# Three middle taps of R from two shared products: their sum and difference added at eviction, the sums of S on GpSimd, T3 as a scalar_tensor_tensor

## The chip, the core and the metric

The kernel runs on one core of a Trainium2 chip, in one launch, everything in float32. The metric is the device time of a run in microseconds; the kernel before took 473.57 us (median of three runs, 473.06 to 473.9). TensorE (PE) multiplies, VectorE (DVE), ScalarE (ACT) and GpSimd (POOL) do the elementwise work, SyncE (SP) issues most DMAs. SBUF holds the tiles, PSUM the results of matmuls.

## The reference, cut to what matters

Four one-dimensional convolutions without a nonlinearity between them, their weights modulated by a style vector per sample, then the residual. 128 samples, 64 channels, 1024 columns.

```python
def _layer(x, style, w, b, mw, mb, typ):
    s = style @ mw.T + mb
    weight = SCALE * w * s[:, None, :, None]
    demod = lax.rsqrt(jnp.sum(weight * weight, axis=(2, 3)) + EPS)
    weight = weight * demod[:, :, None, None]
    if typ == 'same':
        out = jax.vmap(_conv_same)(x, weight) + b[None, :, None]
    elif typ == 'upsample':
        out = jax.vmap(_conv_up)(x, weight.transpose(0, 2, 1, 3)) + b[None, :, None]
        out = _blur(out, 2.0 * blur_k, (1, 1))
    elif typ == 'downsample':
        xb = _blur(x, blur_k, (2, 2))
        out = jax.vmap(_conv_down)(xb, weight) + b[None, :, None]
    return out
...
out = x
for i, typ in enumerate(('same', 'upsample', 'same', 'downsample')):
    out = _layer(out, style, weights[i], biases[i], mod_w[i], mod_b[i], typ)
x = x + out
```

## The kernel before, in words

The four layers are linear, so the kernel first multiplies their weights into one convolution of nine taps per sample (`Wf`, three planes of three taps) and then applies it to x, which is read in three interleaved planes of 342 columns. Four samples are a quad; 32 quads, q = 0 to 31. On the 128 partitions two samples lie one above the other, and a group of four matmuls of 64 rows by 64 columns (two row halves, two column halves) does one tap for all four samples.

**Composing the weights of a quad** has three stages, each a matmul chain into PSUM, then a copy with the sample's scale:

- stage 1 (`stage1_a`, `stage1_b`, L429): the last layer's weights times the third's, in PSUM `psS`. The tile S gets slots 0 to 3 by ScalarE (L400), slots 4 and 5 by VectorE (L482), and GpSimd finishes slot 2 (L485).
- stage 2 (`share`, `stage2_rest`, L507): S times E, the blurred second layer's nine taps, into `psR`: seven blocks of 64 columns. ScalarE evicts them with the scale tC into the tile R (L400, 128x448, one for each row half), and `r_sums` (GpSimd, L639) adds two pairs of R's blocks into R's slots 7 and 8.
- stage 3 (`stage3_b`, `stage3_a`, L622): R times the first layer's weights, in `psA` and `psW`, evicted by ScalarE into `Wf`. VectorE then forms H, the combinations of taps that a fast convolution needs: `combine_a` (H1, L713; the residual's identity in the middle tap, L710, twice; h3, L713) and `combine_b` (three L713).

**The inputs of a quad** (T04, T12, T3) are combinations of x's planes: G by VectorE (`in_g01`, `in_g2`, L713), T3 by VectorE (`in3`, L762), T04 by VectorE (`in04`, L793), the two halves of T12 by GpSimd (`in1` L779, `in2` L784). **The five products** conv0 to conv4 (L814) are twelve matmuls of 342 columns each into `psA` or Y; VectorE's `sum1` (L713) and `sum2` (L713 into Y, L873 into y) combine them, ScalarE writes the outputs (L893).

**Shared products.** Two products of S's sums occur in several blocks of R. `share_sums` (VectorE, L502) adds two pairs of S's slots; `share` multiplies them by E in three groups into a free part of `psA`; `share_copy` (ScalarE, L530) copies the two results, each into two blocks of `psR`, and `stage2_rest` adds the rest of R, 14 groups, on top.

**The order.** Each engine executes its own instructions in the order in which the program writes them; semaphores connect the engines. The prologue has four turns (`early_turn`), then `turn_of(q)` runs for q = 4 to 28, then an epilogue. A turn works on several quads at once, n = q + 1, c = q + 2, s = q + 4: R of quad c, conv2 of q, `r_sums(c)`, `sum2(q)`, `in2(n)`, stage 3 of c, `combine_a(n)`, conv4(q), `combine_b(n)`, conv3(n), stage 1 of s, `in04(n)`, conv0(q), `in_g01(c)`, `share(c + 1)`, conv1(n), `sum1(n)`, `in3(c)`, `in1(c)`. `sharing(q)` holds for q = 5 to 27, 23 turns; only these have the shared products. The tile R has two buffers, S four; `psR`, `psS` and `psW` share one pair of PSUM banks.

Of the kernel before, what the change touches and what calls it, by code (L numbers as in the profile page):

```python
# [48 lines left out]
F32 = mybir.dt.float32  # L49
# [5 lines left out]
C = 64  # L55
# [8 lines left out]
def kernel(  # L64
# [424 lines left out]
    whole, shared_ps = {}, {}  # L489
    later = wsq.rearrange("c l k o -> c (l k) o")  # L490
    Ed, Wd = later[:, :6], later[:, 6:8]

    def tap_differences():

        d = Ed[:, :4].rearrange("c (a b) o -> c a b o", a=2)
        for b in range(2):
            nc_g.tensor_sub(d[:, :, b], E[:, 4 * b : 4 * b + 5 : 4], E[:, 2:7:4])
        nc_g.tensor_sub(Ed[:, 4:], E[:, 3:8:4], E[:, 5:6].to_broadcast([P, 2, C]))

    def share_sums(q):  # L500
        t = whole[q]
        nc_v.tensor_add(t[:, :, 6:8], t[:, :, 1:5:3], t[:, :, 2:6:3])  # L502

    def chain_matmul(dst, weight, st, slots, last=False):
        for r, rows in enumerate(HALF):
            for c, cols in enumerate(HALF):
# [4 lines left out]
                    start=False,  # L511
# [4 lines left out]
    def share(q, ps):  # L516

        at = [NB + 4 + i * C for i in range(3)]
        p12, p34 = ([b[:, i:j] for b in ps] for i, j in zip(at, at[1:]))
        chain_matmul(p12, E[:, 2], chain[q], slice(6, 7))  # L520
        chain_matmul(p34, E[:, 6], chain[q], slice(6, 7))
        chain_matmul(p34, E[:, 5], chain[q], slice(7, 8), True)
        shared_ps[q] = [b[:, at[0] : at[2]] for b in ps]

    def share_copy(q):

        ps = unit(ps_w, f"psR{q}")
        for r in range(2):
            src = shared_ps[q][r].rearrange("c (a o) -> c a o", a=2)
            nc_a.copy(  # L530
                ps[r][:, C : 5 * C].rearrange("c (a b o) -> c a b o", a=2, b=2),
                src[:, :, None, :].to_broadcast([P, 2, 2, C]),
            )
        shared_ps[q] = ps

    def stage2_rest(q):

        ps = shared_ps.pop(q)
        block = lambda i, n=1: [b[:, i * C : (i + n) * C] for b in ps]
        apart = [b[:, : 4 * C].rearrange("c (a b o) -> c a b o", a=2, b=2)[:, :, 0] for b in ps]  # L540
        plan = (
            (apart, E[:, 0], slice(1, 4, 2)),
            (block(1), Ed[:, 0], slice(2, 3)),
            (block(2), Ed[:, 1], slice(1, 2)),
            (block(3), E[:, 2], slice(3, 4)),
            (block(3), Ed[:, 2], slice(2, 3)),
            (block(4), Ed[:, 3], slice(1, 2)),
            (block(4), E[:, 4], slice(3, 4)),
            (block(5, 2), E[:, 8], slice(2, 4)),
            (block(5), E[:, 6], slice(3, 4)),  # L550
            (block(1, 2), E[:, 1], slice(4, 6)),
            (block(2), E[:, 3], slice(4, 5)),
            (block(3), Ed[:, 4], slice(5, 6)),
            (block(4), Ed[:, 5], slice(4, 5)),
            (block(5), E[:, 7], slice(5, 6)),
        )
        for n, (dst, weight, slots) in enumerate(plan):
            chain_matmul(dst, weight, chain[q], slots, n == len(plan) - 1)
        return ps

    def stage2(q, pool=None, engs=(nc_a, nc_a), between=None):
        if q in shared_ps:
# [8 lines left out]
        for r in range(2):  # L571
            scaled_copy(engs[r], flat(t[:, r, :7]), ps[r][:, : 7 * C], tC[:, q, r : r + 1])
# [186 lines left out]
    def in3(q, pairs=BOTH_PAIRS):  # L759
        if q < NQ:  # L760
            X, t = Xs[q % NX], t_tile(q, "T3")
            nc_v.tensor_sub(t[:, pairs, 0, :NJ], plane(X, 3, pairs), plane(X, 1, pairs))  # L762
# [32 lines left out]
    def columns(groups, n):  # L795

        for g in groups:
            for i in range(2) if g < n else (None,):
                yield g, slice(0, NB) if i is None else slice(NB // 2 * i, NB // 2 * (i + 1))

    PIECES = {(0, 3): 3, (0, 1): 3, (0, 2): 3, (1, 3): 2}

    def product(q, m, ps, groups=range(K), alone=False):
# [3 lines left out]
        for g, at in columns(groups, PIECES.get((q, m), 0)):  # L807
            for s, rows in enumerate(HALF):
                for c, cols in enumerate(HALF):
# [4 lines left out]
                    nc.tensor.matmul(  # L814
# [931 lines left out]
```

## Time and profile before

| | before |
|---|---|
| median of 3 runs | 473.57 us (473.06 to 473.9) |
| the profiled execution | 472.43 us |
| its span | 470.6 us |
| instructions | 26974 |
| DMA | 70.79 MB, mean 150 GB/s |
| granted clock of TensorE | 1.00 |

The span is the time from the first to the last instruction that the profiler recorded; the profiled execution's own time is 1.83 us longer. A row of the timeline reads: start in us, duration in us, engine, line of the kernel, operation, output <- input, shape; in square brackets the idle time of the engine before it and what ended it. A row of a line's summary reads: count, then the shortest, median and longest duration in ns. PEld is the load of weights into TensorE, which runs beside its matmuls. In the chain of waits, each piece is a start, a duration and what ran.

### The profile page before, as it was taken

To read this page: it belongs to the slowest core of one execution; us is meant where nothing else is said; L and a number is where in the kernel's file an instruction comes from. 1 tells how busy PE (TensorE), PEld (TensorE's weight loads), DVE (VectorE), ACT (ScalarE), POOL (GpSimd) and SP (SyncE) were. 2 spreads that over 40 slices of the span, in tenths; PEclk is the share of its full clock that TensorE was granted. 3 is DMA by queue.
4 is the path that set the end of the run, shared out by engine and by line. 5 is a ranking of instruction groups with operands and counts; after the bars stand their busy time and mean duration, and the time that the engine had idled before them with its cause. 6 is when DMAs were issued, how large, how long until landed. Compare 5 with 4: busy or idle time off the path is not lost.

```text
span 470.6 us, 26974 instructions
## 1 busy us (share of the span) xinstructions
PE 465.3 (99%) x12036; PEld 339.3 (72%) x12036; DVE 413.4 (88%) x677; ACT 317.9 (68%) x759; POOL 178.4 (38%) x219
## 2 busy tenths in 40 slices
PE   9999999999999999999999999999999999999996
PEld 6997788776677777677766777767677767677653
DVE  5889998879889999998899998889898889999895
ACT  5575666678766678666787667777667677666554
POOL 4535132664348742233322334423233423334410
PEclk9999999999999999999999999999999999999999
DMA  5226455544454544454444455544455535454225
GB/s 178 90 99 200 153 165 169 149 140 145 135 169 154 182 148 138 127 172 156 145 148 136 154 163 177 164 144 152 139 168 155 180 110 168 138 183 154 93 94 183
DMA packets 52836, 70.79 MB, mean 150 GB/s; under 512 B 6128, under 2 KB 50928, under 8 KB 52720
## 3 DMA queue, kind: packets, MB, share of 16 engines
q1 hardware_dynamic: 52496, 68.84, 46.0%
q8 instruction: 94, 1.54, 1.5%
q10 hardware_dynamic: 224, 0.23, 0.1%
q14 instruction: 22, 0.18, 0.1%
HBM read 35.03 MB, written 34.01 MB: 147 GB/s over the span
## 4 chain that ended last, share of the span: by engine, by line
PE 99%; DVE 0%; ACT 0%; issue 0%; DVEq 0%
PE psA L814 47%; PE Y L814 12%; PE psR L507 10%; PE psW L622 8%; PE psA L622 7%; PE psS L429 6%; PE psR L590 5%; PE psA L507 2%; PE psA L1051 1%; PE Y L184 1%; PE psM L221 0%; PE Y L380 0%; PE Y L256 0%; DVE o L895 0%; PE Y L1318 0%; ACT S L400 0%
## 5 line engine op out<-in xcount | busy, mean ns | idle before, releaser
L814 PE MATMUL psA<-T,H 64*64 64x342 f32 (+1 forms) x2392 | 186.5, 438 | 0.1
L814 PEld LDWEIGHTS psA<-T,H 64*64 64x64 f32 x2392 | 88.1, 134 | 49.4 <-issue 2.4
L713 DVE SCALAR_TENSOR_TENSOR G<-X 128x1378 f32<-128x1378 f32 (+2 forms) x65 | 78.3, 1211 | 0.2
L485 POOL TENSOR_TENSOR S<-S 128x128 f32<-128x128 f32 x28 | 21.5, 767 | 138.3 <-ACT S L400 130.9
L779 POOL TENSOR_TENSOR T<-G 128x688 f32<-128x688 f32 x28 | 47.0, 1677 | 70.0 <-DVE G L713 70.0
L814 PE MATMUL psA<-T,Wf 64*64 64x342 f32 x768 | 63.5, 448 | 0.0
L814 PE MATMUL Y<-T,Wf 64*64 64x342 f32 x768 | 62.7, 454 | 0.0
L400 ACT ACTIVATE R<-psR,tC 128x448 f32<-128x448 f32 x63 | 36.6, 631 | 28.7 <-PE psR L507 15.3
L400 ACT ACTIVATE psW<-psA 128x128 f32<-128x128 f32 x100 | 19.3, 268 | 53.6 <-PE psA L622 49.5
L713 DVE SCALAR_TENSOR_TENSOR Y<-m,psA 128x342 f32<-128x342 f32 x62 | 32.2, 519 | 26.3 <-PE psA L814 25.2
L400 ACT ACTIVATE Wf<-psW,t 128x256 f32<-128x256 f32 (+2 forms) x76 | 32.7, 481 | 28.7 <-PE psW L622 28.7
L793 DVE TENSOR_TENSOR T<-G 128x1376 f32<-128x1376 f32 (+1 forms) x34 | 51.7, 1521 | 0.0
L762 DVE TENSOR_TENSOR T<-X 128x688 f32<-128x688 f32 x32 | 50.2, 1570 | 0.0
L784 POOL TENSOR_TENSOR T<-G 128x688 f32<-128x688 f32 x28 | 48.0, 1713 | 0.0
L507 PE MATMUL psR<-S,E 64*64 64x64 f32 (+1 forms) x1472 | 46.0, 238 | 0.0
L429 PEld LDWEIGHTS psS<-wd,w2n 64*64 64x64 f32 x1120 | 33.5, 133 | 14.2
L814 PEld LDWEIGHTS Y<-T,Wf 64*64 64x64 f32 x768 | 28.6, 132 | 18.8
L507 PEld LDWEIGHTS psR<-S,E 64*64 64x64 f32 x1472 | 37.8, 134 | 5.6 <-ACT psR L530 0.2
L893 ACT ACTIVATE o<-psA,tb,td 128x342 f32<-128x342 f32 x63 | 37.3, 651 | 5.0 <-PE psA L814 5.0
L814 PEld LDWEIGHTS psA<-T,Wf 64*64 64x64 f32 x768 | 27.9, 134 | 16.0 <-ACT m L1656 0.2
L893 ACT ACTIVATE o<-y,tb,td 128x342 f32<-128x342 f32 x62 | 38.6, 680 | 0.0
L893 ACT ACTIVATE o<-Y,tb,td 128x342 f32<-128x342 f32 x62 | 36.2, 642 | 2.8 <-PE Y L814 2.0
(186 smaller groups left out, 833.8 us busy)
## 6 DMA issues: line engine op xcount, KB each, us to landing
out<-o SPq DMA_DIRECT2D x191, 172.0 KB, 2.2
X<-in_x SPq DMA_DIRECT2D x150, 172.0 KB, 3.4
X<-in_x SPq DMA_DIRECT2D x14, 516.0 KB, 4.8
par<-in_params SPq DMA_DIRECT2D x3, 192.0 KB, 4.0
Xe<-in_x_ends SPq DMA_DIRECT2D x1, 192.0 KB, 3.0
out<-o ACTq DMA_DIRECT2D x1, 172.0 KB, 2.2
par<-in_params SPq DMA_DIRECT2D x1, 160.0 KB, 2.7
out<-Oc SPq DMA_DIRECT2D x1, 150.0 KB, 1.8
```

The costliest lines, as they stand in the source:

```text
L400: nc_a.activation(dst, src, AF.Copy, scale=f)
L429: nc.tensor.matmul(ps[r][cols, at * C : (at + n) * C], weight[rows], wd[c if r == 0 else 1 - c][rows, taps], start=first, stop=last, skip_ ...
L507: nc.tensor.matmul(dst[r][cols], weight[rows], st[c if r == 0 else 1 - c][rows, slots, :], start=False, stop=last, skip_group_check=True,)
L590: nc.tensor.matmul(ps[r][cols, lo * C : (lo + m) * C], E[rows, e + 2, :], src[rows, a, :], start=(n == 0), stop=(n == 8), skip_group_check ...
L622: nc.tensor.matmul(dst[r][cols], weight[rows], t[rows, c, slots, :], start=first, stop=last, skip_group_check=True,)
L713: nc_v.scalar_tensor_tensor(out, x, f, y, op0=ALU.mult, op1=op)
L762: nc_v.tensor_sub(t[:, pairs, 0, :NJ], plane(X, 3, pairs), plane(X, 1, pairs))
L779: eng.tensor_add(t[:, :, 0, :NJ], plane(g, 2), plane(g, 1))
L784: eng.tensor_sub(t[:, :, 1, :NJ], plane(g, 2), plane(g, 1))
L793: nc_v.tensor_sub(t[:, pairs, :, :NJ], both(a, PL), both(b, 1))
L814: nc.tensor.matmul(ps[s][cols, at], w, Ts[q, tag][rows, c, i, g + at.start : g + at.stop], start=(g == at.start == 0 and (m == 3 or alone) ...
L893: nc_a.activation(dst, src, AF.Identity, bias=add, scale=d3)
```

## The change

Three of R's seven blocks, 2 to 4, now come from the sum and the difference of two products. `share` makes four groups instead of three, with half sums and half differences of E's taps (`Ed`) as weights and with sums and differences of S's slots (`SS`) as the other operand; ScalarE copies the two results u and v out of `psA` with the scale tC, 128x128 for each row half. GpSimd forms `mid` = u + v, u - v, u + v (`share_mid`, two instructions). `stage2_rest` has 11 groups, opens `psR` itself, and is evicted in two parts: ScalarE takes blocks 0, 1, 5 and 6 (one instruction for each row half), VectorE takes blocks 2 to 4 with the scale and adds `mid` in the same instruction.

`share_sums` moves from VectorE, behind `in04`, to GpSimd, right behind `in2`, and has three instructions instead of one. `in3` makes the same difference as a scalar_tensor_tensor with the factor 1. Cutting a convolution's matmuls into two column halves moves inside the loop over the four parts of a group and can end within a group; in 23 more turns the first seven matmuls of conv0 are cut, in turn 11 all twelve, and nine of conv1's in one.

```diff
--- before.py
+++ after.py
@@ -486,80 +486,81 @@
         chain[q] = st
         whole[q] = t
 
-    whole, shared_ps = {}, {}
+    whole, shared = {}, set()
     later = wsq.rearrange("c l k o -> c (l k) o")
-    Ed, Wd = later[:, :6], later[:, 6:8]
+    Ed, Wd = later[:, :9], later[:, 9:11]
 
     def tap_differences():
 
-        d = Ed[:, :4].rearrange("c (a b) o -> c a b o", a=2)
-        for b in range(2):
-            nc_g.tensor_sub(d[:, :, b], E[:, 4 * b : 4 * b + 5 : 4], E[:, 2:7:4])
-        nc_g.tensor_sub(Ed[:, 4:], E[:, 3:8:4], E[:, 5:6].to_broadcast([P, 2, C]))
+        nc_g.tensor_add(Ed[:, :2], E[:, 2:4], E[:, 4:6])
+        nc_g.tensor_sub(Ed[:, 2:4], E[:, 4:6], E[:, 2:4])
+        nc_g.tensor_scalar_mul(Ed[:, :4], Ed[:, :4], 0.5)
+        nc_g.tensor_sub(Ed[:, 4:6], E[:, 0:9:8], E[:, 4:5].to_broadcast([P, 2, C]))
+        nc_g.tensor_sub(Ed[:, 6:8], E[:, 6:8], E[:, 2:4])
+        nc_g.tensor_sub(Ed[:, 8], E[:, 1], E[:, 5])
+
+    SS = const.tile([P, 2, 4, C], F32, name="SS")
+    uv = const.tile([P, 2, 2, C], F32, name="uv")
+    mid = const.tile([P, 2, K, C], F32, name="mid")
 
     def share_sums(q):
         t = whole[q]
-        nc_v.tensor_add(t[:, :, 6:8], t[:, :, 1:5:3], t[:, :, 2:6:3])
-
-    def chain_matmul(dst, weight, st, slots, last=False):
+        nc_g.tensor_add(t[:, :, 0], t[:, :, 1], t[:, :, 3])
+        nc_g.tensor_add(SS[:, :, :2], t[:, :, 0:5:4], t[:, :, 2:6:3])
+        nc_g.tensor_sub(SS[:, :, 2:], t[:, :, 0:6:5], t[:, :, 2:5:2])
+
+    def chain_matmul(dst, weight, st, slots, last=False, first=False):
         for r, rows in enumerate(HALF):
             for c, cols in enumerate(HALF):
                 nc.tensor.matmul(
                     dst[r][cols],
                     weight[rows],
                     st[c if r == 0 else 1 - c][rows, slots, :],
-                    start=False,
+                    start=first,
                     stop=last,
                     skip_group_check=True,
                 )
 
     def share(q, ps):
 
-        at = [NB + 4 + i * C for i in range(3)]
-        p12, p34 = ([b[:, i:j] for b in ps] for i, j in zip(at, at[1:]))
-        chain_matmul(p12, E[:, 2], chain[q], slice(6, 7))
-        chain_matmul(p34, E[:, 6], chain[q], slice(6, 7))
-        chain_matmul(p34, E[:, 5], chain[q], slice(7, 8), True)
-        shared_ps[q] = [b[:, at[0] : at[2]] for b in ps]
-
-    def share_copy(q):
+        sums = [SS[:, r] for r in range(2)]
+        for i in range(4):
+            at = NB + 4 + i // 2 * C
+            chain_matmul([b[:, at : at + C] for b in ps], Ed[:, i], sums, slice(i, i + 1), i == 3)
+        for r in range(2):
+            both = ps[r][:, NB + 4 : NB + 4 + 2 * C]
+            scaled_copy(nc_a, flat(uv[:, r]), both, tC[:, q, r : r + 1])
+
+    def share_mid(q):
+
+        u, v = (uv[:, :, i : i + 1] for i in range(2))
+        twice = [P, 2, 2, C]
+        nc_g.tensor_add(mid[:, :, 0:3:2], u.to_broadcast(twice), v.to_broadcast(twice))
+        nc_g.tensor_sub(mid[:, :, 1:2], u, v)
+
+    def stage2_rest(q):
 
         ps = unit(ps_w, f"psR{q}")
-        for r in range(2):
-            src = shared_ps[q][r].rearrange("c (a o) -> c a o", a=2)
-            nc_a.copy(
-                ps[r][:, C : 5 * C].rearrange("c (a b o) -> c a b o", a=2, b=2),
-                src[:, :, None, :].to_broadcast([P, 2, 2, C]),
-            )
-        shared_ps[q] = ps
-
-    def stage2_rest(q):
-
-        ps = shared_ps.pop(q)
         block = lambda i, n=1: [b[:, i * C : (i + n) * C] for b in ps]
-        apart = [b[:, : 4 * C].rearrange("c (a b o) -> c a b o", a=2, b=2)[:, :, 0] for b in ps]
         plan = (
-            (apart, E[:, 0], slice(1, 4, 2)),
-            (block(1), Ed[:, 0], slice(2, 3)),
-            (block(2), Ed[:, 1], slice(1, 2)),
-            (block(3), E[:, 2], slice(3, 4)),
-            (block(3), Ed[:, 2], slice(2, 3)),
-            (block(4), Ed[:, 3], slice(1, 2)),
-            (block(4), E[:, 4], slice(3, 4)),
+            (block(0, 2), E[:, 0], slice(1, 3)),
+            (block(1), E[:, 2], slice(1, 2)),
+            (block(2), Ed[:, 4], slice(3, 4)),
+            (block(3, 2), Ed[:, 6], slice(1, 3)),
+            (block(4), Ed[:, 5], slice(1, 2)),
             (block(5, 2), E[:, 8], slice(2, 4)),
             (block(5), E[:, 6], slice(3, 4)),
-            (block(1, 2), E[:, 1], slice(4, 6)),
-            (block(2), E[:, 3], slice(4, 5)),
-            (block(3), Ed[:, 4], slice(5, 6)),
-            (block(4), Ed[:, 5], slice(4, 5)),
+            (block(1), E[:, 1], slice(4, 5)),
+            (block(2), Ed[:, 8], slice(5, 6)),
+            (block(4), Ed[:, 7], slice(4, 5)),
             (block(5), E[:, 7], slice(5, 6)),
         )
         for n, (dst, weight, slots) in enumerate(plan):
-            chain_matmul(dst, weight, chain[q], slots, n == len(plan) - 1)
+            chain_matmul(dst, weight, chain[q], slots, n == len(plan) - 1, n == 0)
         return ps
 
     def stage2(q, pool=None, engs=(nc_a, nc_a), between=None):
-        if q in shared_ps:
+        if q in shared:
             ps = stage2_rest(q)
         else:
             ps = opened.pop(q, None)
@@ -569,7 +570,16 @@
             between()
         t = r_pool.tile([P, 2, 9, C], F32, tag="R", name=f"R{q}")
         for r in range(2):
-            scaled_copy(engs[r], flat(t[:, r, :7]), ps[r][:, : 7 * C], tC[:, q, r : r + 1])
+            f = tC[:, q, r : r + 1]
+            if q not in shared:
+                scaled_copy(engs[r], flat(t[:, r, :7]), ps[r][:, : 7 * C], f)
+                continue
+            outer = lambda v: bass.AP(
+                v.tensor, v.offset, [list(v.ap[0]), [5 * C, 2], [1, 2 * C]]
+            )
+            scaled_copy(nc_a, outer(t[:, r, 0]), outer(ps[r][:, :C]), f)
+            inner = flat(t[:, r, 2:5])
+            sum_of(inner, ps[r][:, 2 * C : 5 * C], f, flat(mid[:, r]))
         chain[q] = t
         return ps
 
@@ -759,7 +769,7 @@
     def in3(q, pairs=BOTH_PAIRS):
         if q < NQ:
             X, t = Xs[q % NX], t_tile(q, "T3")
-            nc_v.tensor_sub(t[:, pairs, 0, :NJ], plane(X, 3, pairs), plane(X, 1, pairs))
+            sum_of(t[:, pairs, 0, :NJ], plane(X, 3, pairs), 1.0, plane(X, 1, pairs), ALU.subtract)
 
     def in_g01(q, pairs=BOTH_PAIRS):
         if q < NQ:
@@ -792,33 +802,33 @@
             )
             nc_v.tensor_sub(t[:, pairs, :, :NJ], both(a, PL), both(b, 1))
 
-    def columns(groups, n):
-
-        for g in groups:
-            for i in range(2) if g < n else (None,):
-                yield g, slice(0, NB) if i is None else slice(NB // 2 * i, NB // 2 * (i + 1))
-
-    PIECES = {(0, 3): 3, (0, 1): 3, (0, 2): 3, (1, 3): 2}
+    FIRST_HALVES = {(0, 3): 12, (0, 1): 12, (0, 2): 12, (1, 3): 8, (11, 0): 12, (12, 1): 9}
+
+    def in_halves(q, m):
+        return FIRST_HALVES.get((q, m), 7 if m == 0 and FIRST < q < NQ - 3 else 0)
+
+    ALL, HALVES = (slice(0, NB),), (slice(0, NB // 2), slice(NB // 2, NB))
 
     def product(q, m, ps, groups=range(K), alone=False):
 
         W, H_ = Wq[q]
         tag, i = SLOT[m]
-        for g, at in columns(groups, PIECES.get((q, m), 0)):
+        for g in groups:
             for s, rows in enumerate(HALF):
                 for c, cols in enumerate(HALF):
                     if m in (0, 4):
                         w = W[rows, tap(m // 2, g), c, :]
                     else:
                         w = H_[rows, m - 1, g, c, :]
-                    nc.tensor.matmul(
-                        ps[s][cols, at],
-                        w,
-                        Ts[q, tag][rows, c, i, g + at.start : g + at.stop],
-                        start=(g == at.start == 0 and (m == 3 or alone)),
-                        stop=(g == K - 1),
-                        skip_group_check=True,
-                    )
+                    for at in HALVES if 4 * g + 2 * s + c < in_halves(q, m) else ALL:
+                        nc.tensor.matmul(
+                            ps[s][cols, at],
+                            w,
+                            Ts[q, tag][rows, c, i, g + at.start : g + at.stop],
+                            start=(g == at.start == 0 and (m == 3 or alone)),
+                            stop=(g == K - 1),
+                            skip_group_check=True,
+                        )
 
     def m_tile(tag, q, bufs=1):
         return mpool.tile([P, 2, NB], F32, tag=tag, name=f"{tag}_{q}", bufs=bufs)
@@ -1514,6 +1524,8 @@
                 SLOTS[q - 1][1](A[q - 1])
             sum2(q)
             in2(n, nc_g)
+        if sharing(q):
+            share_sums(c + 1)
         side(TABLES, q)
         for i in range(3):
             load(c + 1, slice(i, i + 1))
@@ -1535,8 +1547,6 @@
                 stage1_a(s)
             copy_m3(n)
         in04(n, PAIR[1] if s == NQ else BOTH_PAIRS)
-        if sharing(q):
-            share_sums(c + 1)
         in_g2(c)
         side(SIDE, q)
         if q in SMALL:
@@ -1551,7 +1561,8 @@
         in_g01(c)
         if sharing(q):
             share(c + 1, banks(q))
-            share_copy(c + 1)
+            share_mid(c + 1)
+            shared.add(c + 1)
         outputs(q, 0)
         if q < LATER_ENDS:
             gather(q)
```

On GpSimd, the place is one sharing turn. Before, the sums of R (L639), `in2` (L784), S's slot 2 (L485) and `in1` (L779) follow each other:

```order
L639 TENSOR_TENSOR R_5321<-R_5321 128x2x128
L784 TENSOR_TENSOR T_18_5259<-G_5189 128x2x344
L485 TENSOR_TENSOR S_5453<-S_5453 128x2x64
L779 TENSOR_TENSOR T_19_5529<-G_5461 128x2x344
L639 TENSOR_TENSOR R_5591<-R_5591 128x2x128
```

In the changed kernel (its lines from L508 on are new, later ones count 10 more) the same stretch reads so, again from the sums of R (L649) to those of the next quad:

```order
L649 TENSOR_TENSOR R_6499<-R_6499 128x2x128
L794 TENSOR_TENSOR T_22_6447<-G_6368 128x2x344
L508 TENSOR_TENSOR S_6361<-S_6361 128x2x64
L509 TENSOR_TENSOR SS<-S_6361 128x2x128
L510 TENSOR_TENSOR SS<-S_6361 128x2x128
L485 TENSOR_TENSOR S_6636<-S_6636 128x2x64
L538 TENSOR_TENSOR mid<-uv 128x2x2x64
L539 TENSOR_TENSOR mid<-uv 128x2x64
L789 TENSOR_TENSOR T_23_6722<-G_6643 128x2x344
L649 TENSOR_TENSOR R_6774<-R_6774 128x2x128
```

Three sums of S (L508 to L510; t0 is the first of them) stand behind `in2` (L794), and the two of `mid` ahead of `in1` (L789).

On VectorE, the place is from the end of one turn (`sum1`, then T3) over `sum2` to h3 of the next. Before:

```order
L713 SCALAR_TENSOR_TENSOR y_19_5795<-psA_5617,m_19_5726 128x684
L762 TENSOR_TENSOR T_20_5797<-X_102 128x688
L713 SCALAR_TENSOR_TENSOR Y<-m_19_5726,psA_5617 128x342 x2
L873 TENSOR_TENSOR y_19_5795<-y_19_5795,psA_5617 128x684
L713 SCALAR_TENSOR_TENSOR H_5619<-Wf_5618 128x384
L710 SCALAR_TENSOR_TENSOR Wf_5618<-idn_156,t_135,Wf_5618 128x64 x2
L713 SCALAR_TENSOR_TENSOR H_5619<-H_5619,Wf_5618 128x384
```

And in the changed kernel:

```order
L723 SCALAR_TENSOR_TENSOR y_19_5893<-psA_5705,m_19_5814 128x684
L723 SCALAR_TENSOR_TENSOR T_20_5895<-X_102 128x688
L723 SCALAR_TENSOR_TENSOR R_5949<-psR_0_5903,tC,mid 128x192
L723 SCALAR_TENSOR_TENSOR R_5949<-psR_1_5904,tC,mid 128x192
L723 SCALAR_TENSOR_TENSOR Y<-m_19_5814,psA_5705 128x342 x2
L883 TENSOR_TENSOR y_19_5893<-y_19_5893,psA_5705 128x684
L723 SCALAR_TENSOR_TENSOR H_5707<-Wf_5706 128x384
L720 SCALAR_TENSOR_TENSOR Wf_5706<-idn_159,t_135,Wf_5706 128x64 x2
L723 SCALAR_TENSOR_TENSOR H_5707<-H_5707,Wf_5706 128x384
```

T3 has its new form, and the two evictions of R's middle blocks stand between it and `sum2`; the sums of S (L502), which stood further on behind `in04`, are gone from this engine.

## The prediction

> **What bounds the kernel now.** I read the page's busy shares and its chain first, then one steady turn by window, by the chain of waits and by the timeline. A turn is one pass of `turn_of`; the change works in the 23 turns with `sharing(q)`, q = 5 to 27.
>
> ```profile
> PE 465.3 (99%) x12036; PEld 339.3 (72%) x12036; DVE 413.4 (88%) x677; ACT 317.9 (68%) x759; POOL 178.4 (38%) x219
> PE 99%; DVE 0%; ACT 0%; issue 0%; DVEq 0%
> ```
> TensorE works for 99% of the span, and the chain that ends last is TensorE's for 99%. The average hides nothing in the middle, as the busy times of one turn's window show (PE, PEld, DVE, ACT, POOL, then clock, DMA share, GB/s):
> ```profile
> 301.90:315.80 13.90, 13.90 (x388) 9.77 (x384) 12.39 (x19) 10.05 (x25) 5.09 (x5) 1.00 0.51 159
> ```
> A turn is 13.90 us, all of it TensorE at full clock; VectorE has 1.51 us left, GpSimd 8.81. The chain of waits gives TensorE's pieces of a turn (start, us, matmul records):
> ```profile
> 283.99 0.35 PE psA L507 x24
> 284.34 1.73 PE psA L814 x24
> 286.07 1.94 PE psR L507 x112
> ...
> 297.89 0.35 PE psA L507 x24
> ```
> No piece waits for another engine. So matmuls removed are time removed, as long as no other engine becomes late; and every microsecond by which one becomes late is added.
>
> **TensorE, removed.** The three groups of `share` (four 64-column matmuls each) take 0.35 us, 0.117 a group. The rest of R had 14 groups, three of them two blocks wide: 17 units in 1.94 us, 0.114 each. After it there are 4 groups and 11 groups, three wide: 14 units. That is 4 x 0.117 + 14 x 0.114 = 2.06 against 2.29 us, **0.22 us less a turn** (rounded down).
>
> **TensorE, added.** Seven of the twelve matmuls of conv0 are cut into column halves in 24 turns. In the prologue a whole conv is cut that way:
> ```profile
> 19.67 1.75 PE psA L814 x48
> ```
> With all halves it takes 1.75 us against 1.73 whole, so 7 of 12 cost 0.01 us a turn. The other end: a column costs 0.114 / 64 = 1.78 ns in the 64-wide groups and 1.73 / 3 / 342 = 1.69 ns in the whole ones, 6% more; on 7/12 of 1.73 us that is 0.06. I take the row of the same operation, 0.01, 0.3 us in all (up to 1.4). Net TensorE: -0.21 us x 23 = -4.8 us.
>
> **ScalarE.** It loses two copies of 128x256 and gains two of 128x128; R's two evictions shrink from 448 to 256 columns.
> ```profile
> L530 ACT COPY psR<-psA x46: 347/360/387, 113.4 to 425.1; 128x256 f32<-128x256 f32 x46
> L400 ACT ACTIVATE psW<-psA x100: 257/266/283, 93.3 to 431.9; 128x128 f32<-128x128 f32 x100
> L400 ACT ACTIVATE Wf<-psW,t x76: 414/472/582, 15.1 to 449.4; 128x256 f32<-128x256 f32 x50, 128x384 f32<-128x384 f32 x13, 128x192 f32<-128x192 f32 x13
> ```
> 0.36 becomes 0.27 (twice), and the eviction pair about 0.84 instead of 1.16 (below): half a microsecond less on an engine that was not late, worth nothing by itself.
>
> **VectorE.** It loses `share_sums`, 0.42, and gains two evictions of 128x192 with one PSUM input.
> ```profile
> L502 DVE TENSOR_TENSOR S<-S x23: 418/419/457, 111.2 to 422.5; 128x256 f32<-128x256 f32 x23
> L482 DVE SCALAR_TENSOR_TENSOR S<-psS,tB,S x56: 275/341/354, 41.9 to 424.6; 128x128 f32<-128x128 f32 x56
> ```
> Between the 0.34 of L482 (128x128) and the 0.54 of one `sum2` half (128x342, 1.07 for two, below) a 128x192 is worth 0.40, so 0.80 for two. They wait for R's outer copies and for `mid`, and stand ahead of `sum2`, which waits for them. There VectorE idles for 1.01 us today (the row at 317.60), so they have room. Where `share_sums` leaves, VectorE only reaches sooner the wait ahead of L482, worth nothing.
>
> **GpSimd.** It gains five sums a turn: of 128 columns (`t0`, `mid` sub) and of 256 (SS add, SS sub, `mid` add). Its own rows for these sizes:
> ```profile
> L639 POOL TENSOR_TENSOR R<-R x24: 725/728/812, 104.0 to 429.6; 128x256 f32<-128x256 f32 x24
> L497 POOL TENSOR_TENSOR wsq<-E x2: 469/473/477, 96.6 to 97.1; 128x128 f32<-128x128 f32 x2
> ```
> Together 3 x 0.73 + 2 x 0.47 = 3.1 us, far under the 8.81 that are free. Room isn't the question; company is. These rows show GpSimd beside VectorE where both inputs of VectorE's instruction lie in SBUF:
> ```profile
> L762 DVE TENSOR_TENSOR T<-X x32: 860/1782/2065, 14.0 to 448.2; 128x688 f32<-128x688 f32 x32
> L710 DVE SCALAR_TENSOR_TENSOR Wf<-idn,t,Wf x64: 272/280/1669, 17.6 to 452.9; 128x64 f32<-128x64 f32 x64
> 17.11 0.56 DVE L713 SCALAR_TENSOR_TENSOR H<-Wf 128x384 f32<-128x384 f32 x1
> 17.19 0.79 POOL L412 TENSOR_TENSOR w3x<-par 128x128 f32<-128x128 f32 x1
> 17.59 0.89 DVE L710 SCALAR_TENSOR_TENSOR Wf<-idn,t,Wf 128x64 f32<-128x64 f32 x2
> 17.95 0.45 POOL L412 TENSOR_TENSOR w2n<-par 128x128 f32<-128x128 f32 x1
> 59.58 1.97 POOL L784 TENSOR_TENSOR T<-G 128x688 f32<-128x688 f32 x1
> 59.96 1.86 DVE L710 SCALAR_TENSOR_TENSOR Wf<-idn,t,Wf 128x64 f32<-128x64 f32 x2
> ```
> They don't run side by side. L762 needs 0.86 alone and 1.78 beside `in1`. The residual, 0.28 alone, takes up to 1.67, and there it is a scalar_tensor_tensor: so **T3's new form changes nothing** (0.86 before; 0.87 for L713 of that size). The order alternates: a GpSimd sum that waits gets in when VectorE's instruction ends. At 17.59 two residuals took 0.89 with two 128x128 sums among them; without company they take 0.47 (305.92, below). So a 128x128 sum costs VectorE's chain **0.21 us**. A 128x256 sum costs between that and its whole 0.73; I add the difference of the durations, 0.73 - 0.45 = 0.28, and take **0.49**.
>
> The Trainium skill, page "SBUF — State Buffer", section "Who interferes with whom", says that a VectorE instruction with two SBUF inputs contends with a GpSimd one that reads SBUF, and that the second waits for the whole instruction of the first. By that the sums would cost 0.45, 0.73 and 0.73, and the forecast reached below would be about 504 us; the two residuals at 17.59 lost 0.42, not 0.9, so I stay with the rows.
>
> **Where the sums fall.** `share_sums` now follows `in2`, and on VectorE H1 (L713), the residuals (L710) and h3 (L713) follow the same `in2`; conv3 waits for h3:
> ```profile
> 305.45 0.55 DVE L713 SCALAR_TENSOR_TENSOR H<-Wf 128x384 f32<-128x384 f32 x1
> 305.92 0.47 DVE L710 SCALAR_TENSOR_TENSOR Wf<-idn,t,Wf 128x64 f32<-128x64 f32 x2
> 306.43 0.56 DVE L713 SCALAR_TENSOR_TENSOR H<-H,Wf 128x384 f32<-128x384 f32 x1
> ...
> 307.37 0.47 PE L814 MATMUL psA<-T,H 64*64 64x342 f32 x4
> ```
> h3 ends at 306.99 and conv3 starts at 307.37: 0.38, of which I leave 0.06 for the signal, **0.32 us of slack**. Into H1, L710, L710, h3 come t0 (0.21), SS add (0.49) and, if it still catches the last residual, SS sub (0.49): 0.70 or 1.19.
>
> **How late in2 is.** The end of a turn and the start of the next, today:
> ```profile
> 311.61 0.53 PE L507 MATMUL psA<-S,E 64*64 64x64 f32 x24
> ...
> 312.43 1.59 DVE L713 SCALAR_TENSOR_TENSOR G<-X 128x1378 f32<-128x1378 f32 x1
> ...
> 314.01 0.87 DVE L713 SCALAR_TENSOR_TENSOR y<-psA,m 128x684 f32<-128x684 f32 x1
> 314.19 1.67 POOL L779 TENSOR_TENSOR T<-G 128x688 f32<-128x688 f32 x1 [2.60 <-DVE G L713]
> 314.80 1.79 DVE L762 TENSOR_TENSOR T<-X 128x688 f32<-128x688 f32 x1
> 315.62 1.91 PE L814 MATMUL psA<-T,H 64*64 64x342 f32 x24
> 315.89 1.16 ACT L400 ACTIVATE R<-psR,tC 128x448 f32<-128x448 f32 x2 [0.66 <-PE psR L507]
> 317.06 0.98 PEld L622 LDWEIGHTS psA<-R,w0s 64*64 64x64 f32 x24
> 317.13 0.72 POOL L639 TENSOR_TENSOR R<-R 128x256 f32<-128x256 f32 x1 [1.28 <-ACT R L400]
> 317.60 1.07 DVE L713 SCALAR_TENSOR_TENSOR Y<-m,psA 128x342 f32<-128x342 f32 x2 [1.01 <-PE psA L814]
> 317.81 1.65 POOL L784 TENSOR_TENSOR T<-G 128x688 f32<-128x688 f32 x1
> 319.35 0.55 DVE L713 SCALAR_TENSOR_TENSOR H<-Wf 128x384 f32<-128x384 f32 x1
> ```
> H1 starts at 319.35, 0.11 before `in2` is recorded as ended, and takes its usual 0.55: today it comes just as `in2` lets go. With the change the products are out at about 312.26, `uv` at 312.9, and `mid` add then stands behind `in_g01`, which runs to 314.02. It ends near 314.7; `mid` sub gives way near 315.0; VectorE's in3, ready at 314.88, goes next, to 315.8; and `in1` after it, to 317.35. On TensorE the turn is 0.23 us early by then (conv2 at 315.39). R: outer copies 315.66 to 316.5, the inner ones end at 316.95; stage3_b's weights come at 317.06 - 0.23 = 316.83 and its matmuls 0.3 later, so at most 0.1 us is lost there, and I take none. `r_sums` waits for `in1` until 317.4, 0.27 us later than today on a turn that is 0.23 early: `in2` is **0.50 us late**. Were `in1` done in time, R alone would set it: 316.95 against 317.05, 0.13 late.
>
> **Sum.** conv3 then waits lateness + sums - 0.32: 0.51 or 0.88 with the two sums, 1.00 or 1.37 with three. Less 0.21, that is 0.30, 0.67, 0.79 and 1.16 us a turn. Nothing here tells the four corners apart, so I take their middle, 0.73: x 23 = 16.8 us. The profiled execution (472.43 us, 1.14 under the median) becomes 489.2, the median 473.57 becomes **490**. The corners give 480 to 500.
>
> **Rivals.** *The sums cost nothing where they stand (faster).* If VectorE's instructions follow each other so closely that GpSimd gets in only after h3, or if the new form escapes the exclusion, and `in2` is no more than 0.3 late, TensorE's gain shows whole: 473.57 - 4.8 = 468.8. It decides at 0.32 + 0.21 = 0.53 us of delay a turn. For it: H1 and L762's neighbours show 0.55 and 0.86 wherever GpSimd rests, and GpSimd has time to wait. Against it: the 17.59 row is this very chain with sums among it, and 59.96 shows the residual behind `in2`.
> *Only t0 gets in.* With 0.13 to 0.50 of lateness and 0.21, the wait is 0.02 to 0.39: -0.19 to +0.18 a turn, 469 to 478, about no change at its middle.
> *in1 goes ahead of in3.* Then in3, and R's inner columns behind it, are late: `in1` from 315.0 to 316.4, in3 to 317.3, R at 318.1, 1.2 us behind what stage3_b wants, with the sums still to come: over 1.5 us a turn, 508 or more. Against it: at 314.80 VectorE's in3 would now be the one that waits.
> *The change doesn't do what it says:* T3's form is no faster by itself and `share_sums` frees VectorE where it idles. I count that as part of every case.
>
> **How the numbers follow.** My case has 0.57, the faster rival 0.24, t0 alone 0.11, `in1` first 0.08. The range runs from 468 (the faster rival) to 503 (the top corner and a little of stage3_b's wait or the halves); it leaves out the last rival and edges, less than 2 in 10. My case's own range is 480 to 500. About 0.2% (0.95 us) is what a measurement of this kernel can tell from no change: faster 0.28 (the faster rival and a third of t0 alone), same 0.04, slower 0.68.
>
> **What would show it.** Right: TensorE idle ahead of conv3 for 0.5 to 1.4 us a turn, released by VectorE's H; L710 in sharing turns at 0.5 or more instead of 0.28; L639 released by GpSimd's own `in1`, not by R; share and rest of R at 2.06 us. Wrong: turns of 13.7 us with TensorE still full, sums recorded at 1 us or more because they wait for h3; or TensorE idle ahead of stage3_b, on R. My forecast falls if GpSimd's sums do not split the chain from H1 to h3.

## The result, and the profile after

The changed kernel took **495.89 us** (median of 4 runs, 495.52 to 496.36) against 473.6 us before; the ratio is 1.0471, 95% interval 1.0456 to 1.0487. It is slower by 22.3 us, 0.97 us for each of the 23 sharing turns. The forecast was 490 us, with a range of 468 to 503.

On the page of the changed kernel, TensorE's share falls and GpSimd's grows; the chain that ends last, which was TensorE's alone, now runs through VectorE for 18% of the span. The third line is from the view of the waits:

```profile
PE 471.9 (96%) x12032; PEld 396.5 (80%) x12032; DVE 444.6 (90%) x700; ACT 311.2 (63%) x759; POOL 293.0 (59%) x337
PE 40%; DVE 18%; issue 2%; ACT 1%; DVEq 0%
PE psA L824 <- DVE H L723: 13.5, 24, 0.8
```

In 24 turns conv3 waits for VectorE's H, as the forecast had it. The timeline of one turn shows why (start, duration, engine, line):

```profile
316.16 0.45 POOL L539 TENSOR_TENSOR mid<-uv 128x128 f32<-128x128 f32 x1
316.56 0.86 DVE L723 SCALAR_TENSOR_TENSOR T<-X 128x688 f32<-128x688 f32 x1
316.58 2.36 POOL L789 TENSOR_TENSOR T<-G 128x688 f32<-128x688 f32 x1
318.89 0.73 POOL L649 TENSOR_TENSOR R<-R 128x256 f32<-128x256 f32 x1
319.58 1.65 POOL L794 TENSOR_TENSOR T<-G 128x688 f32<-128x688 f32 x1
320.77 0.88 DVE L723 SCALAR_TENSOR_TENSOR H<-Wf 128x384 f32<-128x384 f32 x1
321.19 0.77 POOL L508 TENSOR_TENSOR S<-S 128x128 f32<-128x128 f32 x1
321.57 0.67 DVE L720 SCALAR_TENSOR_TENSOR Wf<-idn,t,Wf 128x64 f32<-128x64 f32 x2
322.04 0.79 POOL L509 TENSOR_TENSOR SS<-S 128x256 f32<-128x256 f32 x1
322.27 0.97 DVE L723 SCALAR_TENSOR_TENSOR H<-H,Wf 128x384 f32<-128x384 f32 x1
322.79 1.04 POOL L510 TENSOR_TENSOR SS<-S 128x256 f32<-128x256 f32 x1
323.17 1.08 DVE L723 SCALAR_TENSOR_TENSOR H<-Wf 128x384 f32<-128x384 f32 x1
323.39 1.96 PE L824 MATMUL psA<-T,H 64*64 64x342 f32 x24 [0.53 <-DVE H L723]
```

`in1` (L789) lets T3 go ahead and takes 2.36 us, `r_sums` (L649) comes right behind it, and `in2` (L794) still runs when VectorE reaches H1, which takes 0.88 instead of 0.55. Then the sums (L508, L509, L510) and VectorE's instructions alternate: the two residuals take 0.67 instead of 0.47, h3 0.97 instead of 0.56, and the third sum delays only the H behind h3. TensorE stands idle for 0.53 us. In a full stream its records overlap, so the loss is read from the starts, first in the kernel before, then in the changed one on both sides of the conv3 above:

```profile
307.26 0.29 PE L622 MATMUL psW<-R,w0s 64*64 64x64 f32 x8
307.37 1.91 PE L814 MATMUL psA<-T,H 64*64 64x342 f32 x24
309.10 0.73 PE L429 MATMUL psS<-wd,w2n 64*64 64x128 f32 x24
...
322.57 0.29 PE L632 MATMUL psW<-R,w0s 64*64 64x64 f32 x8
325.13 0.76 PE L429 MATMUL psS<-wd,w2n 64*64 64x128 f32 x24
```

conv3 starts 0.11 us behind the row ahead of it before and 0.82 after: it is 0.71 us late. From its own start to the next row it takes 1.73 us before and 1.74 after.

This turn is 14.5 us long. A turn that follows side work of VectorE (two additions for the ends of the rows, L1150, 0.88 us together, in q = 14 to 16) is 15.17 us long; the windows of one of each, the second with such a pair of additions in it as well:

```profile
332.07:346.56 14.49, 13.96 (x387) 12.12 (x383) 13.27 (x19) 9.77 (x26) 9.46 (x10) 1.00 0.48 147
257.56:272.73 15.17, 14.30 (x390) 11.73 (x386) 14.48 (x22) 9.79 (x27) 10.15 (x10) 1.00 0.45 143
```

The fourth number is VectorE's busy time: 14.48 of 15.17 us in the second, with the time in it that its instructions wait for GpSimd. Before, the same turns took 13.90 and 13.9 to 14.1 us. Behind the side work `in_g01` comes later, and `mid` meets its start and takes 2.22 us instead of 1.47. `in1` and `in2` follow, and in the next turn VectorE reaches H1 into a much later `in2`:

```profile
268.61 0.88 DVE L1150 TENSOR_TENSOR Ve<-We 128x320 f32<-128x320 f32 x2
269.89 2.22 POOL L538 TENSOR_TENSOR mid<-uv 128x256 f32<-128x256 f32 x1 [1.93 <-ACT uv L400]
269.93 1.58 DVE L723 SCALAR_TENSOR_TENSOR G<-X 128x1378 f32<-128x1378 f32 x1
...
275.40 1.65 POOL L794 TENSOR_TENSOR T<-G 128x688 f32<-128x688 f32 x1
276.13 1.34 DVE L723 SCALAR_TENSOR_TENSOR H<-Wf 128x384 f32<-128x384 f32 x1
```

H1 waits 0.8 us here, not 0.33. Turn by turn between the two profiled executions, twelve turns grew by 0.42 to 0.61 us, one by 0.70 and eleven by 0.85 to 2.2. The three turns behind side work (q = 15 to 17) are among the eleven, while q = 14, which only starts it, grew by 0.57; turns with tables on GpSimd (q = 7 to 9) are among them too. That each of the eleven has such a reason isn't shown.

### The profile page after: what moved, and what is told of

It is laid out like the page before. It is cut to its first block, busy times and chain, and to the rows that moved or that the text cites. A ratio compares the mean times of both kernels' runs of the same rounds, so it can differ in the third digit from the quotient of the medians.

```text
span 493.7 us, 27122 instructions
## 1 busy us (share of the span) xinstructions
PE 471.9 (96%) x12032; PEld 396.5 (80%) x12032; DVE 444.6 (90%) x700; ACT 311.2 (63%) x759; POOL 293.0 (59%) x337
## 4 chain that ended last, share of the span: by engine, by line
PE 40%; DVE 18%; issue 2%; ACT 1%; DVEq 0%
PE psA L824 28%; DVE H L723 7%; PE psR L515 5%; DVE Y L723 4%; PE psS L429 3%; DVE y L883 3%; DVE Wf L720 2%; PE psA L515 1%; PE Y L824 1%; PE psA L1061 1%; DVE y L723 1%; PE psR L600 1%; PE psW L632 0%; DVE R L723 0%; ACT o L903 0%
## 5 line engine op out<-in xcount | busy, mean ns | idle before, releaser
L824 PEld LDWEIGHTS psA<-T,H 64*64 64x64 f32 x2410 | 118.4, 133 | 41.7 <-issue 11.0
L485 POOL TENSOR_TENSOR S<-S 128x128 f32<-128x128 f32 x28 | 15.1, 539 | 90.9 <-ACT S L400 83.5
L824 PE MATMUL psA<-T,Wf 64*64 64x171 f32 (+1 forms) x1114 | 67.2, 363 | 0.0
L789 POOL TENSOR_TENSOR T<-G 128x688 f32<-128x688 f32 x28 | 57.5, 2055 | 11.3 <-DVE G L723 11.3
L538 POOL TENSOR_TENSOR mid<-uv 128x256 f32<-128x256 f32 x23 | 37.3, 1620 | 37.9 <-ACT uv L400 37.9
L723 DVE SCALAR_TENSOR_TENSOR H<-Wf 128x384 f32<-128x384 f32 x64 | 58.9, 921 | 0.0
L794 POOL TENSOR_TENSOR T<-G 128x688 f32<-128x688 f32 x28 | 47.8, 1709 | 0.0
L824 PEld LDWEIGHTS psA<-T,Wf 64*64 64x64 f32 x1114 | 44.9, 133 | 2.8 <-ACT m L1667 0.2
L723 DVE SCALAR_TENSOR_TENSOR H<-H,Wf 128x384 f32<-128x384 f32 x64 | 43.5, 680 | 2.1
L400 ACT ACTIVATE R<-psR,tC 128x256 f32<-128x256 f32 (+1 forms) x63 | 29.2, 514 | 23.0 <-PE psR L600 13.2
L400 ACT ACTIVATE S<-psS,tBn 128x256 f32<-128x256 f32 x56 | 23.5, 471 | 29.8 <-PE psS L429 29.8
L632 PEld LDWEIGHTS psA<-R,w0s 64*64 64x64 f32 x1000 | 35.2, 133 | 7.3 <-DVE R L723 3.1
```

The costliest lines, as they stand in the source:

```text
L400: nc_a.activation(dst, src, AF.Copy, scale=f)
L485: nc_g.tensor_add(t[:, :, 2], t[:, :, 2], t[:, :, 0])
L538: nc_g.tensor_add(mid[:, :, 0:3:2], u.to_broadcast(twice), v.to_broadcast(twice))
L632: nc.tensor.matmul(dst[r][cols], weight[rows], t[rows, c, slots, :], start=first, stop=last, skip_group_check=True,)
L723: nc_v.scalar_tensor_tensor(out, x, f, y, op0=ALU.mult, op1=op)
L789: eng.tensor_add(t[:, :, 0, :NJ], plane(g, 2), plane(g, 1))
```

## The experiments

All are compared by the medians of runs beside the kernel before (473.6 us), and by the length of a turn in one profiled execution of each: the distance from the start of one eviction of R by ScalarE to the next, in a stretch of plain turns and in the three turns behind side work (q = 15 to 17, their median).

| kernel | median us | plain turn | behind side work |
|---|---|---|---|
| before | 473.57 | 13.90 | 13.94 |
| the change | 495.89 | 14.50 | 15.17 |
| no_sums | 477.52 | 13.89 | 14.17 |
| no_mid | 491.91 | 14.49 | 15.23 |
| no_both | 475.78 | 13.90 | 14.24 |
| before_pool | 479.47 | 14.18 | 14.18 |
| gate_h3 | 497.34 | 14.40 | 15.40 |
| dve_sums | 490.31 | 14.18 | 15.37 |
| t3_tt | 496.24 | 14.50 | 15.18 |
| no_halves | 497.64 | 14.41 | 15.81 |
| none_in3 | 476.06 | 13.76 | 14.23 |
| none_in3_whole | 475.45 | 13.67 | 14.24 |
| after_in3 | 495.20 | 14.51 | 15.28 |
| before_halves | 476.19 | 13.99 | 14.01 |

**no_sums, no_mid, no_both: what each group of GpSimd's new instructions costs.**

```diff
-        if sharing(q):
+        if q == FIRST + 1:
             share_sums(c + 1)
...
-            share_mid(c + 1)
+            if q == FIRST + 1:
+                share_mid(c + 1)
```

The first edit alone is no_sums:

> The changed kernel with the three sums of S on GpSimd made in the first sharing turn only; the later 22 turns multiply the old sums (that part of the computation is left out). My theory: the sums stand between H1 and h3 and cost VectorE's chain 0.6 us a turn; without them only in2's lateness is left, which today shows as a longer H1 (0.34 us over its 0.55 in plain turns, 0.80 in turns with extra work on VectorE) against 0.32 of slack, so nothing in plain turns and about 0.5 in some eight others: 472 to 476. Rival (in1 and in2 late behind mid are the whole cause): 485 or more. Rival (VectorE and GpSimd together have no room left on what they share, wherever the sums stand): also down, to 472 to 478; told apart by the kernel that moves the sums behind h3.

It took 477.52 us, 1.5 above my range and inside that of the second rival, which gate_h3 below is to tell apart: 18.4 of the 22.3 us are gone, and a plain turn is back at 13.89. `share` doesn't wait for the sums themselves in the changed kernel: TensorE's waits there name none of them. The second edit alone is no_mid:

> The changed kernel with the two instructions of mid on GpSimd made in the first sharing turn only; the later turns add the old mid (that part is left out). My theory: in1 then goes right after in_g01 and is done before R, in2 is 0.13 us late at most, the sums still cost 0.6, less 0.32 of slack: conv3 waits 0.4 us a turn, 0.2 net, 476 to 481. Rival (the sums are the whole cause): 493 to 496, no change. Rival (in2's lateness is the whole cause): 469 to 471.

It took 491.91 us, only 4.0 less, and a plain turn is as long as with `mid`; none of the three forecasts holds. Its timeline shows what took the place of `mid`:

```profile
327.67 1.66 POOL L789 TENSOR_TENSOR T<-G 128x688 f32<-128x688 f32 x1 [2.96 <-PE psA L824]
328.47 1.59 DVE L723 SCALAR_TENSOR_TENSOR T<-X 128x688 f32<-128x688 f32 x1
329.99 0.73 DVE L723 SCALAR_TENSOR_TENSOR R<-psR,tC,mid 128x192 f32<-128x192 f32 x2
330.80 0.72 POOL L649 TENSOR_TENSOR R<-R 128x256 f32<-128x256 f32 x1 [1.47 <-DVE R L723]
```

Now `in1` goes first and T3 waits for it; R's inner blocks are queued behind T3 on VectorE, and `r_sums` waits for R. With `mid`, T3 goes first and `in1` is late. Either way `r_sums` and `in2` are late. Both edits together:

> The changed kernel with the sums of S and mid both made in the first sharing turn only. My theory: nothing of GpSimd's is late, only TensorE's saving of 0.21 us a turn is left: 468.8, 468 to 470, and TensorE never idle ahead of conv3. Rival (TensorE's new groups or the cut halves cost more than counted, or R's two evictions in a row are late): 471 to 476.

475.78 us, 2.2 more than before (ratio 1.0054, interval 1.0033 to 1.0074): without the sums and `mid`, TensorE's saving still didn't show. The rival held, and the last four kernels look for what ate it.

**before_pool: one sum, in the other kernel.** VectorE's one sum goes to GpSimd behind `in2`; the old call goes.

```diff
-        nc_v.tensor_add(t[:, :, 6:8], t[:, :, 1:5:3], t[:, :, 2:6:3])
+        nc_g.tensor_add(t[:, :, 6:8], t[:, :, 1:5:3], t[:, :, 2:6:3])
...
             in2(n, nc_g)
+        if sharing(q):
+            share_sums(c + 1)
```

> The kernel before with its one sum of S (128x256) moved from VectorE to GpSimd, right behind in2, and nothing else changed. My theory: one sum of that size costs the chain from H1 to h3 0.41 to 0.49 us where in2 is on time; less 0.32 of slack 0.1 to 0.17 us a turn: 476 to 477.5. Rival (slack covers it, or GpSimd waits until h3 is through): 473.6, or a little less.

It took 479.47 us, 5.9 more (ratio 1.0124, interval 1.0094 to 1.0154). The timeline has the sum among the residuals, which take 0.95 instead of 0.47 (0.49 was the price of a 128x256 sum):

```profile
351.96 1.07 POOL L502 TENSOR_TENSOR S<-S 128x256 f32<-128x256 f32 x1
352.36 0.95 DVE L710 SCALAR_TENSOR_TENSOR Wf<-idn,t,Wf 128x64 f32<-128x64 f32 x2
353.34 0.56 DVE L713 SCALAR_TENSOR_TENSOR H<-H,Wf 128x384 f32<-128x384 f32 x1
```

In the chain of waits of the same kernel, conv3 follows:

```profile
354.05 1.96 PE psA L814 x24
```

The mechanism is the forecast one; the turn grew by 0.28, not by 0.1 to 0.17. h3 ends at 353.90 and conv3 starts 0.15 later, so 0.15 and not 0.06 of the 0.38 us was never slack: the 0.48 that the residuals lose, less 0.23 of slack, is 0.25. conv3's 1.96 us is no price of its own. In a full stream the chain counts a piece from the end of the one before it (1.73), after an idle time from its own start; from start to start conv3 takes 1.74 here too.

**gate_h3: the same sums, held back until h3 is written.** The wait is one more GpSimd instruction, a copy of 128x1 that takes 0.45 us; the old call goes.

```diff
+    seen = const.tile([P, 1], F32, name="seen")
-    def share_sums(q):
+    def share_sums(q, after):
         t = whole[q]
+        nc_g.tensor_copy(seen, after)
...
             combine_a(n)
             conv4(q)
+        if sharing(q):
+            share_sums(c + 1, Wq[n][1][:, 2, 0, 0, :1])
```

> The changed kernel with the three sums of S held back on GpSimd until h3 is written (a copy of one column of h3 to a scratch tile goes ahead of them); everything is computed. My theory: the chain from H1 to h3 is free of them, so conv3 waits only for in2's lateness, but the 1.2 us that the sums take from VectorE fall on combine_b and the inputs behind it, and whatever of it VectorE's idle time ahead of L482 (about 0.6) doesn't absorb makes in_g01, mid, in1 and in2 later: 480 to 489. Rival (only the place counts, VectorE has room): 476 to 479, as without the sums. Rival (VectorE and GpSimd are simply full together): 493 to 497.

497.34 us, no gain at all, outside my range and 0.3 above that of the second rival. Some 5 us of it are one turn of 20.76 us, in which the sums came behind GpSimd's tables and `share` waited for them; but a plain turn, too, is 14.40 us. Its rows:

```profile
337.87 1.35 DVE L726 SCALAR_TENSOR_TENSOR H<-Wf 128x384 f32<-128x384 f32 x1
339.14 0.47 DVE L723 SCALAR_TENSOR_TENSOR Wf<-idn,t,Wf 128x64 f32<-128x64 f32 x2
339.64 0.56 DVE L726 SCALAR_TENSOR_TENSOR H<-H,Wf 128x384 f32<-128x384 f32 x1
...
341.57 0.97 DVE L726 SCALAR_TENSOR_TENSOR H<-H,Wf 128x384 f32<-128x384 f32 x1
342.46 2.12 DVE L806 TENSOR_TENSOR T<-G 128x1376 f32<-128x1376 f32 x1
```

The residuals and h3 are short again. The sums now delay combine_b's last H and T04 (2.12 instead of 1.58); VectorE comes later to `in_g01`, `mid` behind it, then `in1` and `in2`, and H1 waits 0.80 instead of 0.33 us. What was taken from one place came back at the other, one turn later.

**dve_sums: the three sums on VectorE, behind in04.** In the diff, `nc_g` becomes `nc_v` in `share_sums`, and its call moves back to its old place.

```diff
         in04(n, PAIR[1] if s == NQ else BOTH_PAIRS)
+        if sharing(q):
+            share_sums(c + 1)
         in_g2(c)
```

> The changed kernel with the three sums of S on VectorE, behind in04, where the kernel before had its one sum; everything is computed. My theory: they take about 0.28 + 0.42 + 0.42 = 1.1 us there, 0.7 more than the one sum before, which the idle 0.63 ahead of L482 takes up in plain turns but not in turns with extra work on VectorE: 477 to 483, near the kernel without the sums (477.5). Rival (the two engines are full together): 490 to 496.

490.31 us, ratio 1.0344 (1.0324 to 1.0364): at the edge of the rival's numbers. A plain turn is 0.3 us longer than without the sums, since H1 waits 0.63 us for `in2` (it takes 1.18); in turns behind side work, 15.37 us, VectorE's instructions and their waits for GpSimd fill 15.20.

**t3_tt and no_halves: the two small parts undone.**

```diff
-            sum_of(t[:, pairs, 0, :NJ], plane(X, 3, pairs), 1.0, plane(X, 1, pairs), ALU.subtract)
+            nc_v.tensor_sub(t[:, pairs, 0, :NJ], plane(X, 3, pairs), plane(X, 1, pairs))
...
-        return FIRST_HALVES.get((q, m), 7 if m == 0 and FIRST < q < NQ - 3 else 0)
+        return FIRST_HALVES.get((q, m), 0)
```

> The changed kernel with T3 made by tensor_tensor as before. My theory: the form changes nothing, since both forms were kept waiting in the trace of before: 495 to 497. Rival (the new form is taken ahead of GpSimd's sums more easily): 498 or more.

496.24 us: the form makes no difference, to 0.1%.

> The changed kernel without the cut halves in the steady turns (conv0 whole; the prologue's cuts and the one of conv1 stay). My theory: 0.01 to 0.06 us a turn less on TensorE, and TensorE waits ahead of conv3 in most turns anyway: 494.5 to 496. Rival (the cuts serve something, such as the loading of TensorE's instructions): 497 or more.

497.64 us. That is the rival's number, but a plain turn is 0.09 us shorter without the halves; one behind side work is 0.64 longer. There the order of requests tips over:

```profile
271.66 0.73 POOL L538 TENSOR_TENSOR mid<-uv 128x256 f32<-128x256 f32 x1 [1.85 <-ACT uv L400]
271.79 2.06 DVE L723 SCALAR_TENSOR_TENSOR G<-X 128x1378 f32<-128x1378 f32 x1
272.34 1.81 POOL L539 TENSOR_TENSOR mid<-uv 128x128 f32<-128x128 f32 x1
274.12 1.64 POOL L789 TENSOR_TENSOR T<-G 128x688 f32<-128x688 f32 x1
274.54 1.95 DVE L723 SCALAR_TENSOR_TENSOR T<-X 128x688 f32<-128x688 f32 x1
```

`mid` starts 0.13 us ahead of `in_g01`, which takes 2.06 instead of 1.58; the second half of `mid` waits for it; `in1` goes ahead of T3, and R is late behind T3. With the halves `mid` starts 0.04 us ahead in such a turn, and it is `mid` that waits. This is the forecast's rival "in1 goes ahead of in3", decided by a tenth of a microsecond.

**none_in3, none_in3_whole, after_in3, before_halves: what ate TensorE's saving.** T3 is written ahead of stage1_b.

```diff
         if s < NQ:
+            in3(c)
             stage1_b(s)
...
         sum1(n)
-        if s < NQ:
-            in3(c)
```

On top of no_both:

> The kernel without the later sums of S and mid (no_both, 475.8; both made in the first sharing turn only), with in3 written ahead of stage1_b, so that VectorE makes T3 in its idle time before L482 and not between sum1 and R's inner blocks. My theory: what ate TensorE's saving in no_both is R's inner eviction, queued on VectorE behind T3, which waits for in1; without that in2 is on time: 469 to 472. Rival (the serial eviction, ScalarE then VectorE, is late by itself, or VectorE's idle time ahead of L482 is too short): 474 to 478.

> The same, with conv0 whole in the steady turns (no halves). My theory: the halves cost TensorE 0.08 us a turn (a plain turn took 14.41 us without and 14.49 with them), so 1 to 2 us less than none_in3: 467 to 471. Rival (the halves keep TensorE's rounds in step): not less, or more.

476.06 and 475.45 us: by the medians both forecasts fail, and the first is inside its rival's range. Part of it is that the edit also reached the first steady turn, q = 4, 1.0 us longer in both since it waits there for L482; part are the turns behind side work, which stayed at 14.23 and 14.24. But the plain turns answer the question: 13.76, and 13.67 without halves. The chain of the latter, through one turn:

```profile
317.92 1.59 PE psR L515 x88
319.51 1.73 PE psA L824 x24
...
325.16 1.73 PE psA L824 x24
...
329.39 0.47 PE psA L515 x32
329.86 1.73 PE psA L824 x24
331.59 1.45 PE psR L515 x77
```

Here TensorE is full again (conv3 1.73), share and the rest of R take 0.47 + 1.59 = 2.06 us, the number of the forecast, and the turn is 0.23 shorter than before. So T3's place cost 0.13 to 0.14 us a turn and the halves 0.09.

In before_halves the kernel before gets the new loop and its cuts, and nothing else:

> The kernel before with the changed kernel's halves alone (seven of conv0's twelve matmuls cut in the steady turns, the loop over halves inside). My theory: TensorE is the bound there, so the cost shows whole: 0.02 to 0.08 us in 24 turns, 474.1 to 475.5. Rival (they cost nothing or help): 473.6 or less.

476.19 us, ratio 1.0060 (1.0043 to 1.0076): 2.6 us, 0.1 a turn, above what I had expected. In the chain, conv0 with its seven cuts takes 1.78 us instead of 1.73, and the stretch behind it, up to conv1, 0.64 instead of 0.58. In turn 11, where all twelve are cut, conv0 takes 1.84:

```profile
325.92 1.78 PE psA L814 x34
198.34 1.84 PE psA L814 x46
```

In after_in3 the changed kernel, with all its sums, gets T3 at the new place:

> The changed kernel, all computed, with in3 written ahead of stage1_b. My theory: in2 comes on time and H1's wait of 0.34 us goes, the sums of S between H1 and h3 stay (0.6 us against about 0.24 of slack): some 0.3 us a turn less, 484 to 491, still slower than before. Rival (VectorE and GpSimd are full together and the wait only moves, to in_g01 and mid): 494 to 498.

495.20 us, ratio 1.0458 (1.0439 to 1.0476), 0.7 less than the change: the rival held. H1 waits only 0.16 us there, but `mid` still queues behind `in_g01`, the sums still split the chain to h3, and three times TensorE's weight loads ahead of R's matmuls wait for L482, which stands behind T3, 1.2 us in all. conv3's idle time shrinks from 0.53 to 0.36 us in a plain turn, but in the chain the rest of R and conv2 grow, 1.62 and 1.92 us instead of 1.53 and 1.77; why they do is open. No version of the change that computes everything came near the kernel before (490 to 498 us).

## Why the prediction was right, point by point

- **TensorE's saving: right as counted, 0.23 us a turn**, shown by none_in3_whole (13.67 against 13.90). It never showed in the changed kernel.
- **The halves: mis-sized.** I took 0.01 us a turn from a piece of the prologue's chain, with 0.06 as the other end; they cost 0.09 to 0.10. A part of it is the reading: by its starts that prologue conv takes 1.80 us, 0.07 more than a whole one, and 7/12 of that is 0.04. All twelve cut cost 0.11 us in conv0's own piece in before_halves, seven 0.05, so it isn't only the change from cut to whole that costs; what the cost consists of is open.

```profile
19.45 1.98 PE L814 MATMUL psA<-T,H 64*64 64x171 f32 x48
21.25 0.18 PE L965 MATMUL Y<-cc,wsum 64*64 64x16 f32 x2
```

- **The sums in the chain to h3: right.** I named t0 and SS add as certain and SS sub as open, at 0.21 and 0.49. Measured: t0 0.20 in the residuals, SS add 0.41 in h3, SS sub behind h3, the corner with two sums. Without the sums 18.4 of the 22.3 us go; with the sums behind h3 nothing goes (gate_h3). So the forecast had the path right on which they cost here, but that place is not what makes them dear. By the page "SBUF — State Buffer", section "Who interferes with whom", of the Trainium skill, VectorE would have lost a sum's whole 0.45 and 0.73, an estimate; it lost 0.20 and 0.41, so the rows were the better price. The section's rule that such pairs exclude each other agrees with the alternating rows above.
- **Slack: 0.24 instead of 0.32**, since the signal from h3 to conv3 takes 0.15 and not 0.06, for which the forecast showed no row.
- **in2's lateness: the mechanism half right.** H1 waits 0.33 in plain turns, within my 0.13 to 0.50. But I put it down to `mid`, with 0.13 as the case without it. The step "were in1 done in time, R alone would set it" failed: no_mid shows that R then comes late behind T3.
- **The sum of a plain turn:** 0.33 + 0.20 + 0.41 - 0.24 = 0.70, and conv3 starts 0.71 late; with -0.23 and +0.09 that is 0.56, measured 0.60. My corner for two sums and a late `in2` was 0.67, the middle that I took 0.73.
- **What made 490 into 496:** I took one plain turn for all 23. With side work, VectorE, which before found room for it in its idle time, comes later to `in_g01`, `mid`, `in1` and `in2`, and in the turn behind it H1 waits 0.5 us more: such turns grew by 1.05 to 1.28 us instead of 0.60, and eleven turns by 0.85 or more. Plain turns throughout, 24 times 0.60, would have made 488; that 490 came within 6 us is in part luck, since a plain turn was put 0.13 too high.
- **The rivals:** the faster one fell: every version of the change that has the sums is slower than before. That T3's form does nothing is shown by t3_tt. "in1 ahead of in3" was real, and no_halves and no_mid show it.

What the forecast lacked is that there was a second limit, on VectorE and GpSimd together. gate_h3 and dve_sums show the wait going elsewhere when the sums are moved. That the two are full together, rather than merely badly ordered, is argued from these two and not shown: an order that fits all of it into 13.9 us wasn't found, nor was every order tried.

## What to carry to other kernels

Where two engines exclude each other, count their exclusive work together before giving one of them more: GpSimd had 8.8 us a turn free here, and 1.9 us of sums on it cost more than 18 us in all. Moving such work behind the waiting chain returns the wait by another path if the engine that loses the time feeds the same chain a turn later. And read the turns with extra work too: a forecast from the plain turn alone was 6 us short, and would have been 8 short with the plain turn right.

## What the runs showed of the hardware that was not expected

- An idle time in TensorE's record is less than what was lost: in the full stream conv3's row ends 0.18 us after the next one has started (307.37 + 1.91 against 309.10), so 0.53 us of idle time ahead of it are 0.71 us by the starts.
- Seven matmuls of 342 columns cut in halves cost 0.09 to 0.10 us a turn where TensorE is the bound (before_halves, none_in3 against none_in3_whole), of which 0.05 show in the piece of their own convolution (1.78 against 1.73).
- A GpSimd sum of 128x256 holds up VectorE for 0.41 to 0.48 us, less than the 0.73 that it takes by itself.
